# Layer 0's gate folded beside the projection's last queries, and all additions to the expert weights issued beside the attention

## The chip, the cores and the metric

The kernel runs on one core of a Trainium2 chip. Its metric is the device time of one execution in microseconds (us). Three runs of the kernel before took 980.25, 982.1 and 984.28 us; the median is 982.1. The engines are named as in the profile: PE is TensorE (PEld its weight loads), DVE is VectorE, ACT is ScalarE, POOL is GpSimd and SP is SyncE. A q behind a name (SPq, ACTq) is an engine's instruction queue, from which DMAs are issued.

## What is computed

Two transformer-like layers run over 8 batches of 256 tokens with 512 features, all in float32. This change lies in layer 0:

```python
# layer 0, attention: 8 heads of 64, 4 key/value groups, window of 256 keys, paged cache
q, k, v = x @ Wq.T, x @ Wk.T, x @ Wv.T          # RMS norm and rotation on q and k
k_blocks, v_blocks = cache with the 256 new rows of each batch written in
o = softmax(q k^T / 16, masked to the window) v
a = o @ Wo.T
# layer 0, feed-forward: top 2 of 8 experts
logits = clip(a @ gate_w.T, -50, 50)
rw = softmax(top 2 of logits)
weighted = (softmax(expert_atom_weights) @ atoms) * sigmoid(importance)   # 8 x 4096
out = a @ W.T + for each of 4096 places (row, col): out[row] += a[col] * sum_k rw_k * weighted[expert_k, place]
x = x + out
# layer 1: low-rank adapters on a linear layer, then a mixture of 8 GELU experts, added to x
```

Two rearrangements matter here. The logits are `o @ (Wo.T @ gate_w.T)`, so the kernel folds the gate through the output weights once (into `gwo`, 512 x 8) and multiplies attention outputs by that. And each expert's sparse update is added into a dense matrix of its own: `delta_d` in DRAM first receives W for all 8 experts, then the 4096 weighted values are added to it at their places, 128 places by one indirect DMA, 32 DMAs in all.

## The kernel before

**Order.** The program is written as Python loops; a list scheduler orders the instructions of each engine, by program order as their priority and by what is ready in its own model, so instructions of neighbouring steps interleave. Each engine then runs its list strictly in order, and waits at semaphores. A tile pool that is opened in memory of a closed one waits for the readers and writers of what lay there.

**Projection (L1147 to L1350).** PSUM is split into `psq` (3 banks) and `psd` (3 banks with tag psd, and one each for `pw0` and `pw1`). For 16 tiles of 128 tokens, `keys_values` multiplies (L1158), normalises and rotates keys and stores keys and values to `kv_new` (L1175). Beside it, `sum_same` (L1276) makes the values that are to be added to the weights (`sums`), and `find_places` their rows (`put_i`). From tile 8 on, six of the 32 additions are issued there, one to a tile (L1337, `add_delta` at L1127, on POOL). Loads of `wq`, `woT` and `gw` go through `later` (L1307), which writes one element of the tile from a late result, so that the load on SP can't run ahead. Then `gather_new(0)` fetches the new rows of batch 0, and the queries of batches 0 and 1 are made: `query_rows` (L1092, products at L1096) and `queries_turned` (L1114, transposes at L1121).

**Fold (L1490).** After the projection's pools are closed, each of four 128-column blocks of `woT` is transposed (L1497) and copied by ACT (L1499), and four products with 8 moving columns (`gw`) are accumulated (L1501). Four copies write `gwo` (L1509). It uses banks of the attention's pools.

**Attention (L1526 to L1568).** For batch b: the cache rows of batch b + 2 are gathered by POOL (4 DMAs from the old cache, 4 from `kv_new`, L1058), its queries are made (L1366, L1096, with a power on POOL at L1109 for `roots`), the sums in DRAM are started (L1520, L1523), and 128 queries attend (L1408 scores, L1423 mask and maximum, L1439 exponent, L1453 and L1457 transposes, L1462 values). Then `prepared` turns the keys of batch b + 1 (L1378, L1381) and builds its masks, five additions to `delta_d` are issued on POOL from `entries` (L1551 to L1561; one is left for batch 5), and the other 128 queries attend. `gate_rows` (L1479) and `output_rows` (L634) follow. In the last two batches the finished weights are read back (`raw`, L615) and laid out (L622).

**Layer 1** folds its gate with the helper `seen_through` (L114), which this change will use for layer 0 too. Its product is written as

```python
nc.tensor.matmul(
    acc[o * BW : (o + 1) * BW, :], gate[:, o, :], wn, start=True, stop=True
)
```

that is, 32 stationary columns (8 gates and zeros) and 512 moving ones; the four partial sums land in four groups of 32 partitions of one bank, which is copied, transposed and reduced by DVE (L134).

Of the kernel before, what the change touches and what calls it, by code (L numbers as in the profile page):

```python
# [11 lines left out]
F32 = mybir.dt.float32  # L12
# [7 lines left out]
P = 128  # L20
B, T, D = 8, 256, 512
# [3 lines left out]
KC = D // P  # L25
# [6 lines left out]
E = 8  # L32
# [3 lines left out]
NSC = NS // P  # L36
# [45 lines left out]
def two_layer_kernel(ctx: ExitStack, tc: tile.TileContext, io: dict, out: bass.AP):  # L82
    nc = tc.nc
# [14 lines left out]
    ident = const.tile([P, P], F32, name="ident")  # L98
# [4 lines left out]
    RK, BW = 16, 32  # L103
# [496 lines left out]
    woT = op.tile([P, KC, D], F32, name="woT")  # L600
    gwo = op.tile([P, KC, E], F32, name="gwo")
# [44 lines left out]
    with ExitStack() as att:  # L646
        ap = att.enter_context(tc.tile_pool(name="ap", bufs=1))
# [7 lines left out]
        sums = place_ap.tile([P, NSC, E], F32, name="sums")  # L655
# [9 lines left out]
        minus_half = ap.tile([P, 1], F32, name="minus_half")  # L665
        nc.gpsimd.memset(minus_half, -0.5)

        gw = ap.tile([P, KC, E], F32, name="gw")
        epss = ap.tile([P, 2], F32, name="epss")
        nc.gpsimd.memset(epss[:, 0:1], EPS)  # L670
        nc.gpsimd.memset(epss[:, 1:2], EPS / (SCALE * SCALE))
# [455 lines left out]
        def add_delta(k, values):  # L1127

            nc.gpsimd.indirect_dma_start(
                out=delta_d,  # L1130
                out_offset=bass.IndirectOffsetOnAxis(ap=put_i[:, k : k + 1], axis=0),
                in_=values,
                in_offset=None,
                bounds_check=D * D + P - 1,
                oob_is_err=True,
                compute_op=ALU.add,
            )
# [2 lines left out]

        roots = ap.tile([P, NT, H], F32, name="roots")

        BESIDE = 6
        LATER = 5


        with proj:  # L1147
# [3 lines left out]
            psd = proj.enter_context(tc.tile_pool(name="psd", bufs=3, space=PSUM))  # L1151
# [68 lines left out]
            for j in range(2):  # L1220
                for k in range(NSQ):
                    for h in range(2):
# [5 lines left out]
                            start=True,  # L1228
# [78 lines left out]
            def later(tile, src, rs):  # L1307

                nc.scalar.copy(tile[:, 0, :1], rs[:, :1])
                nc.sync.dma_start(tile, src)  # L1310

            FIRST = 8
            summed = placed = 0
            for i in range(LEAD, NT):
                rs = keys_values(i)
                if i == LEAD:
                    with_gains(qcos, qsin, "q_scale")
                    rot.close()
                base_weights(i)
                if i == 3:  # L1320
                    later(wq, wsrc[:, :, :512], rs)
                if i == 8:
                    later(woT, io["woT"].rearrange("(c p) o -> p c o", p=P), rs)
                    later(gw, io["gate0T"].rearrange("(c p) e -> p c e", p=P), rs)
                if i == 4:
                    find_blocks(psd, rs)
                if i in (6, 8, 10):
                    find_rows(i // 2 - 3)
                if i in (9, 11):
                    gather_old(i // 2 - 4)  # L1330
                for k in range(summed, min(summed + 3, NSC)):
                    sum_same(k)
                    summed = k + 1
                if summed - placed >= 8 or i == NT - 1:
                    find_places(range(placed, summed))
                    placed = summed
                if i >= FIRST and i - FIRST < BESIDE:  # L1337
                    add_delta(i - FIRST, sums[:, i - FIRST, :])
            gather_new(0)

            qq = proj.enter_context(tc.tile_pool(name="qq", bufs=2, side="right"))
            QTs = {}
            for b in range(2):
                rows = [
                    query_rows(
                        i, blocks[NTB][:, :, i * P : (i + 1) * P], psq, "pkv", qq, early=True
                    )
                    for i in range(2 * b, 2 * b + 2)
                ]
                QTs[b] = queries_turned(rows, psd, "psd")  # L1350


        otp = ost.enter_context(tc.tile_pool(name="otp", bufs=1, side="right"))
# [132 lines left out]
            nc.vector.tensor_scalar(lg0[:, i, :], pg, 50.0, -50.0, ALU.min, ALU.max)  # L1486

        AHEAD = 2

        with ExitStack() as fold:  # L1490
            fo = fold.enter_context(tc.tile_pool(name="fo", bufs=1))
            pgos = [ps_s.tile([P, 2, 512], F32, name="pgo", tag="ps") for j in range(KC // 2)]
            pgo = [pgos[k // 2][:, k % 2, :E] for k in range(KC)]
            for d in range(KC):
                pw = ps_o.tile([P, KC, P], F32, name="pw", tag="misc")
                for k in range(KC):
                    nc.tensor.transpose(pw[:, k, :], woT[:, k, d * P : (d + 1) * P], ident)  # L1497
                won = fo.tile([P, D], F32, name="won")
                nc.scalar.copy(won, pw.rearrange("p c r -> p (c r)"))  # L1499
                for k in range(KC):  # L1500
                    nc.tensor.matmul(  # L1501
                        pgo[k],
                        won[:, k * P : (k + 1) * P],
                        gw[:, d, :],
                        start=(d == 0),
                        stop=(d == KC - 1),
                    )
            for k in range(KC):
                nc.scalar.copy(gwo[:, k, :], pgo[k])  # L1509

        gather_new(1)
        ready = prepared(0, kv_rows[0])
        zero = wop.tile([P, D], F32, name="zero")
# [12 lines left out]
        for b in range(B):  # L1526
# [21 lines left out]
            now = ready  # L1548
            if b + 1 < B:
                ready = prepared(b + 1, kv_rows[b + 1])  # L1550
            ks = range(BESIDE + LATER * b, min(BESIDE + LATER * (b + 1), NSC))  # L1551
            if ks:

                held = bp.tile([P, 1], F32, name="held")
# [567 lines left out]
```

## Time and profile before

| | |
|---|---|
| median of three runs | 982.1 us (980.25 to 984.28) |
| profiled execution | 983.58 us, of which its span is 981.7 |
| mean granted TensorE clock | 0.967 |
| projection's last query product ends | 108.31 us |
| first scores of the attention | 133.42 us |
| last addition to `delta_d` issued | 313.0 us |
| additions issued by POOL | 6 from `sums` (94.2 to 116.1), 26 from `entries` (135.3 to 313.0) |

Times are microseconds from the start of the span of one profiled execution. "Busy" is what an engine worked; the bracket behind an instruction says how long its engine idled before it and which result ended the wait. The granted clock is TensorE's speed as a share of full speed. One float32 product shows as two records, a transpose as one. Instructions on PE are pipelined, so the distance between the starts of neighbours tells more than the length of one.

### The profile page before, as it was taken

The numbers are of one execution on the slowest core, as the hardware profiler recorded it, in microseconds if no ns is written. First come the engines' busy times: TensorE is split into PE (matmuls) and PEld (weight loads), VectorE is DVE, ScalarE is ACT, GpSimd is POOL, SyncE is SP. The second block draws the span as 40 slices with busy tenths as digits, with TensorE's granted clock in tenths as the row PEclk, the third lists the DMA queues.
The fourth block names the chain that finished last, engine by engine and source line by source line (L and its number), as shares of the span: only waits on it lengthen the run. The fifth ranks groups of instructions, "written<-read, shape, count | busy, mean of one in ns | idle before, by whom it ended". The sixth has DMA issues, their size and how long they took to land. (4 is left out here: it accounts for less than half of the span.)

```text
span 981.7 us, 14436 instructions
## 1 busy us (share of the span) xinstructions
PE 914.2 (93%) x4897; PEld 511.9 (52%) x4897; DVE 455.7 (46%) x1477; ACT 372.5 (38%) x958; POOL 357.2 (36%) x333
## 2 busy tenths in 40 slices
PE   6998889999999998897999997999599999999995
PEld 3554646556556565545433333545277777753332
DVE  5786789758548576583211111471012222323332
ACT  3675447547557489651111112410111111112321
POOL 2631655654554300123666652000223333333211
PEclk9898789999999999997999999999799999999998
DMA  6696494423441202256997766981433444343322
GB/s 192 216 320 236 123 306 143 115 59 82 118 126 28 93 19 70 84 195 226 344 308 139 126 111 144 357 315 43 171 74 67 70 73 73 65 75 62 49 28 37
DMA packets 74238, 134.63 MB, mean 137 GB/s; under 512 B 17309, under 2 KB 22941, under 8 KB 74032
## 3 DMA queue, kind: packets, MB, share of 16 engines
q0 software_dynamic: 25088, 43.68, 23.5%
q1 hardware_dynamic: 38496, 74.57, 21.9%
q10 hardware_dynamic: 10576, 15.39, 4.3%
q8 instruction: 42, 0.69, 0.3%
q14 instruction: 36, 0.29, 0.1%
HBM read 89.95 MB, written 52.56 MB: 145 GB/s over the span
## 5 line engine op out<-in xcount | busy, mean ns | idle before, releaser
L575 DVE COPY xsT<-pa 128x512 f32<-128x512 f32 x68 | 46.8, 688 | 155.6 <-PE pa L569 148.5
L533 POOL DMA_INDIRECT xs<-g_d,token_i_l x34 | 35.3, 1037 | 229.4 <-PE pa L569 129.4
L2014 DVE TENSOR_TENSOR y<-py,b 64x512 f32<-64x512 f32 (+1 forms) x46 | 31.7, 690 | 185.8 <-PE py L547 122.2
L1998 ACT ACTIVATE hs<-pu,b 128x64 f32<-128x64 f32 (+1 forms) x184 | 46.2, 348 | 185.8 <-PE pu L1972 144.4
L556 PE MATMUL py<-delta,xsT 128*64 128x512 f32 (+1 forms) x416 | 94.8, 598 | 0.0
L1439 ACT ACTIVATE s<-s,mx,roots 128x384 f32<-128x384 f32 x128 | 89.7, 705 | 12.2 <-DVE mx L1435 11.3
L1972 PE MATMUL pu<-xsT,w 128*128 128x128 f32 x704 | 82.9, 276 | 0.0
L1972 PEld LDWEIGHTS pu<-xsT,w 128*128 128x128 f32 x704 | 80.9, 193 | 0.4 <-issue 0.4
L547 PE MATMUL py<-w,hs 128*128 128x512 f32 x176 | 79.3, 593 | 0.0
L1158 PE MATMUL pkv<-wkv,xb 128*128 128x512 f32 x128 | 66.9, 648 | 8.5 <-DMA wkv<-wqkvT 8.5
L580 POOL DMA_INDIRECT out<-y,token_i_l x34 | 54.0, 1587 | 55.6 <-DVE y L2015 51.2
L1462 PE MATMUL po<-pT,kv 128*64 128x128 f32 x768 | 66.0, 283 | 7.1 <-ACT pT L1457 7.1
L1423 DVE CUSTOM_DVE_ANT_0 s<-ps,mask 128x384 f32<-128x384 f32 x128 | 67.1, 551 | 11.8 <-PE ps L1408 10.0
L1788 ACT ACTIVATE y<-py,weight_l 128x512 f32<-128x512 f32 x34 | 23.4, 688 | 126.1 <-PE py L556 86.9
L1462 PEld LDWEIGHTS po<-pT,kv 128*64 128x64 f32 x768 | 46.0, 136 | 43.1 <-ACT pT L1457 35.8
L580 POOL DMA_INDIRECT sums_d<-y,token_i_l x34 | 53.9, 1586 | 31.4 <-ACT y L1788 13.8
L1408 PE MATMUL ps<-KT,QT 64*128 64x384 f32 x256 | 59.1, 541 | 4.2 <-DVE mx L1423 4.0
L1457 ACT COPY pT<-pp 128x384 f32<-128x384 f32 x128 | 55.9, 478 | 16.7 <-PE pp L1453 15.8
L1453 PE MATMUL pp<-ident,s 128*128 128x128 f32 x384 | 59.9, 283 | 2.5 <-DVE s L1450 2.4
L569 PEld LDWEIGHTS pa<-ident,xs 128*128 128x128 f32 x272 | 32.7, 145 | 53.8 <-issue 48.4
L569 PE MATMUL pa<-ident,xs 128*128 128x128 f32 x272 | 43.6, 286 | 18.1 <-DMA xs<-g_d,token_i_l 11.4
L1096 PE MATMUL pq<-wq,xb 128*128 128x512 f32 x128 | 59.7, 614 | 0.0
(385 smaller groups left out, 1546.4 us busy)
## 6 DMA issues: line engine op xcount, KB each, us to landing
delta_d<-spread SPq DMA_DIRECT2D x16, 512.0 KB, 4.8
raw<-delta_d SPq DMA_DIRECT2D x16, 512.0 KB, 4.6
w<-fc_w SPq DMA_DIRECT2D x8, 1024.0 KB, 19.4
w<-fc_w SPq DMA_DIRECT2D x16, 512.0 KB, 17.3
part<-sums_d SPq DMA_DIRECT2D x32, 256.0 KB, 4.8
xb<-xT SPq DMA_DIRECT2D x5, 1024.0 KB, 6.4
sums_d<-zero SPq DMA_DIRECT2D x18, 256.0 KB, 5.4
kv_new<-kvt ACTq DMA_DIRECT2D x16, 256.0 KB, 2.7
```

The source lines that it names most:

```text
L547: nc.tensor.matmul(py, xT[:, k, :], of_expert(experts[0])(weights(k)), start=(k == 0), stop=(k == KC - 1),)
L556: lambda k=k, h=h: nc.tensor.matmul(py[h * HR : (h + 1) * HR, :], xT[:, k, h * HR : (h + 1) * HR], of_expert(experts[h])(weights(k)), star ...
L569: nc.tensor.transpose(dst[:, k, :], src[:, k * P : (k + 1) * P], ident)
L580: nc.gpsimd.indirect_dma_start(out=sum_d, out_offset=bass.IndirectOffsetOnAxis(ap=token_i[:, s : s + 1], axis=0), in_=y, in_offset=None, b ...
L1096: nc.tensor.matmul(pq, xcols[:, k, :], wq[:, k, :], start=(k == 0), stop=(k == KC - 1))
L1158: nc.tensor.matmul(pkv, xb[:, k, cols], wkv[:, k, :], start=(k == 0), stop=(k == KC - 1),)
L1408: lambda r=r: nc.tensor.matmul(pss[r], QT[r * HD : (r + 1) * HD, m, t * P : (t + 1) * P], KT[r * HD : (r + 1) * HD, u, t * P : t * P + WU] ...
L1423: nc.vector.tensor_tensor_reduce(out=s, in0=pss[r], in1=mask[:, t, :], scale=1.0, scalar=NEG, op0=ALU.add, op1=ALU.max, accum_out=mx[:, r ...
L1439: nc.scalar.activation(ss[r], ss[r], AF.Exp, bias=mx[:, r : r + 1], scale=root[:, r : r + 1], accum_out=sm[:, r : r + 1],)
L1453: nc.tensor.transpose(pp[:, c * P : (c + 1) * P], s[:, c * P : (c + 1) * P], ident)
L1462: lambda c=c, r=r: nc.tensor.matmul(po[r * HD : (r + 1) * HD, :], kvs[t + c][:, v0 + r * HD : v0 + (r + 1) * HD], pTs[r][:, c * P : (c + 1 ...
L1972: nc.tensor.matmul(pu[:, c, :], w1[:, k, plan.full[s], c * P : (c + 1) * P], xsT[:, k, :], start=(k == 0), stop=(k == KC - 1),)
```

## The change

`gw` is made 32 columns wide with zeros behind the 8 gates, and the load writes only the 8. The fold of L1490 is removed; `seen_through` is called in the projection's scope instead, after all query products of batches 0 and 1 and ahead of the turning of batch 1's queries. It uses the bank tagged `pw0` for its sums, the three `psd` banks for transposes, ACT for its copies and the pool `qq` for its SBUF tiles. The six additions of the projection loop are dropped there, and the attention's loop issues six to a batch from batch 0 on, so batches 0 to 4 take 30 and batch 5 the last two.

```diff
-        gw = ap.tile([P, KC, E], F32, name="gw")
+        gw = ap.tile([P, KC, BW], F32, name="gw")
+        nc.gpsimd.memset(gw, 0.0)
...
-        BESIDE = 6
-        LATER = 5
+        LATER = 6
...
-                nc.sync.dma_start(tile, src)
-
-            FIRST = 8
+                nc.sync.dma_start(tile[:, :, : src.shape[-1]], src)
+
...
-                if i >= FIRST and i - FIRST < BESIDE:
-                    add_delta(i - FIRST, sums[:, i - FIRST, :])
             gather_new(0)
 
             qq = proj.enter_context(tc.tile_pool(name="qq", bufs=2, side="right"))
-            QTs = {}
+            QTs, rows = {}, {}
             for b in range(2):
-                rows = [
+                rows[b] = [
...
-                QTs[b] = queries_turned(rows, psd, "psd")
+                if b == 0:
+                    QTs[b] = queries_turned(rows[b], psd, "psd")
+
+            seen_through(
+                gwo,
+                lambda o: [woT[:, k, o * P : (o + 1) * P] for k in range(KC)],
+                gw,
+                qq,
+                lambda name, shape: psd.tile(
+                    shape, F32, name=name, tag="pw0" if name == "acc" else "psd",
+                    bufs=1 if name == "acc" else 3,
+                ),
+                nc.scalar.copy,
+            )
+            QTs[1] = queries_turned(rows[1], psd, "psd")
...
-        with ExitStack() as fold:
-            fo = fold.enter_context(tc.tile_pool(name="fo", bufs=1))
-            pgos = [ps_s.tile([P, 2, 512], F32, name="pgo", tag="ps") for j in range(KC // 2)]
-            pgo = [pgos[k // 2][:, k % 2, :E] for k in range(KC)]
-            for d in range(KC):
-                pw = ps_o.tile([P, KC, P], F32, name="pw", tag="misc")
-                for k in range(KC):
-                    nc.tensor.transpose(pw[:, k, :], woT[:, k, d * P : (d + 1) * P], ident)
-                won = fo.tile([P, D], F32, name="won")
-                nc.scalar.copy(won, pw.rearrange("p c r -> p (c r)"))
-                for k in range(KC):
-                    nc.tensor.matmul(
-                        pgo[k],
-                        won[:, k * P : (k + 1) * P],
-                        gw[:, d, :],
-                        start=(d == 0),
-                        stop=(d == KC - 1),
-                    )
-            for k in range(KC):
-                nc.scalar.copy(gwo[:, k, :], pgo[k])
...
-            ks = range(BESIDE + LATER * b, min(BESIDE + LATER * (b + 1), NSC))
+            ks = range(min(LATER * b, NSC), min(LATER * (b + 1), NSC))
```

The helper that both folds now call:

```python
def seen_through(dst, blocks, gate, pool, banks, copy, **tags):
    acc = banks("acc", [P, D])
    for o in range(KC):
        pw = banks("pw", [P, KC, P])
        for k, src in enumerate(blocks(o)):
            nc.tensor.transpose(pw[:, k, :], src, ident)
        wn = pool.tile([P, D], F32, name="wn", **tags)
        copy(wn, pw.rearrange("p c r -> p (c r)"))
        nc.tensor.matmul(
            acc[o * BW : (o + 1) * BW, :], gate[:, o, :], wn, start=True, stop=True
        )
    parts = pool.tile([P, D], F32, name="parts", **tags)
    nc.scalar.copy(parts, acc)
    pt = banks("pt", [P, KC, P])
    for d in range(KC):
        nc.tensor.transpose(pt[:, d, :], parts[:, d * P : (d + 1) * P], ident)
    nc.vector.tensor_reduce(
        dst,
        pt.rearrange("p d (o c) -> p d c o", o=KC)[:, :, :E, :],
        AX.X,
        ALU.add,
    )
```

## The prediction, as it was made before the change was run

> **What bounds the kernel now.** I read first the table of busy time and the 40 slices, then windows over the stages, then the waits and the order of time around the one place the change moves.
>
> ```profile
> PE 914.2 (93%) x4897; PEld 511.9 (52%) x4897; DVE 455.7 (46%) x1477; ACT 372.5 (38%) x958; POOL 357.2 (36%) x333
> ...
> PEclk9898789999999999997999999999799999999998
> ```
>
> TensorE is busy 93% of the span, so time is won where TensorE idles or runs at a lowered clock. The clock row dips at the fifth slice (98 to 123 us). That is where the projection ends, the gate is folded (L1490 to L1509) and the attention has not begun. Windows of TensorE alone there (busy us, then granted clock, DMA share, GB/s):
>
> ```profile
> 108.00:110.00 2.00, 0.75 (x5) 1.00 0.35 42
> 110.00:112.00 2.00, 0.63 (x4) 0.86 1.07 358
> 112.00:114.00 2.00, 1.85 (x9) 0.50 0.98 331
> 122.00:124.00 2.00, 2.00 (x11) 0.50 0.58 152
> 126.00:128.00 2.00, 2.00 (x4) 0.50 0.98 280
> 128.00:130.00 2.00, 2.00 (x6) 0.88 1.02 343
> ```
>
> See two losses: from 108 to 112 TensorE does 1.4 us of work in 4, and from 111.5 to 128.3 it runs at clock 0.50. In order of time on TensorE:
>
> ```profile
> 104.71 3.60 PE L1096 MATMUL pq<-wq,xb 128*128 128x512 f32 x8
> 108.15 0.60 PE L1121 MATMUL pt<-ident,qr 128*128 128x128 f32 x4
> 110.84 0.63 PE L1121 MATMUL pt<-ident,qr 128*128 128x128 f32 x4 [2.10 <-DVE qr L1090]
> 112.15 1.97 PE L1497 MATMUL pw<-ident,woT 128*128 128x128 f32 x8 [0.68 <-ACT QT L1124]
> ...
> 124.43 9.05 PE L1096 MATMUL pq<-wq,xb 128*128 128x512 f32 x16
> 133.42 1.56 PE L1408 MATMUL ps<-KT,QT 64*128 64x384 f32 x8
> ```
>
> The last query product of the projection ends at 108.31 and the first scores start at 133.42: 25.1 us. Three parts: 3.8 us to the first transpose of the fold (mostly waits: batch 1's turned queries wait 2.10 for VectorE, the fold 0.68 for the copy that frees the projection's PSUM), 12.3 us of fold with 8 transposes of the keys (pk) among it, all at clock 0.50, and 9.0 us of batch 2's queries, the first 3.9 at 0.50. From 163 to 313 TensorE is busy 35.0 to 38.4 of 36 to 39 us a stage, so what the front gains is carried on.
>
> **The fold's work.** Removed: 16 transposes and 32 records of an 8-column product (16 matmuls, two passes each), four copies L1499, four L1509. At clock 0.50 a round (4 transposes, 8 records) takes 2.61 us (115.72 to 118.33), four 10.4. At full clock it would be 5.2, half of that. Added: the same transposes, four products of 512 columns on 32 stationary ones, one copy of the sum, four transposes, one reduction. The same helper already runs for layer 1, at clock 1.00:
>
> ```profile
> 606.58 1.05 PE L126 MATMUL acc<-wn,gw 128*32 128x512 f32 x4 [2.11 <-ACT wn L125]
> ...
> 609.76 1.05 PE L126 MATMUL acc<-wn,gw 128*32 128x512 f32 x2
> ...
> 611.11 1.05 PE L126 MATMUL acc<-wn,gw 128*32 128x512 f32 x2
> 612.89 0.66 PE L133 MATMUL pt<-ident,parts 128*128 128x128 f32 x4 [0.73 <-ACT parts L130]
> 613.93 1.09 PE L1839 MATMUL pt<-ident,part 128*128 128x128 f32 x8 [0.38 <-DVE gwc L134]
> ```
>
> One product alone holds TensorE 0.98 us (609.76 to 610.74); two side by side also 0.98 (606.58 to 607.57). So four cost 2.0 to 3.9, with 20 transposes at 0.116 (8 in 0.93, 151.92 to 152.85) 4.3 to 6.2 us: as much TensorE work as the old fold at full clock. Nothing is gained by the arithmetic; the gain must come from the place.
>
> The page "TensorE: Matmul & The Clock Gate" of the Trainium skill (section "Back-to-back issue gap") speaks against the new form: it gives 1 to 64 moving columns about 60 cycles and 512 about 518. By it four wide products (2072 cycles a pass) cost twice the sixteen narrow ones (960), about 0.9 us more over two passes at full clock (an estimate); the rows above give -1.4 to +0.5 us (2.0 to 3.9 against the 3.4 of half the 8-record stretch, 1.72, four times). I stay with the rows.
>
> **The new front, step by step, at full clock.** The transposes of woT need only woT (landed at 85) and a bank, so they fit the waits before 108.3 or follow it.
> - First round if nothing is hoisted: 0.46 transposes, about 0.2 wait, copy 0.59 (the L1499 row), 0.2 wait: first product at 109.7; if hoisted, 108.3.
> - Three rounds of 0.98 + 0.46 between first and last product: last one starts at 112.6 to 114.0. Batch 1's second query tile (ready at 110.7) is turned inside this, its waits covered.
> - Tail from the last product's start to the next user of TensorE: 2.82 us (611.11 to 613.93: copy, 4 transposes, reduction). The closing projection pool holds pk until then: 115.4 to 116.9.
> - pk 0.93: 116.4 to 117.8.
> - Batch 2's queries: their input is issued by SP at 108.46, just after the last read of the projection's block, and lands within 5.8 us (longest of that row): 114.3, so it does not hold them. 16 records take 7.13 us at full clock (row of 173.93). First scores at 123.5 to 124.9 against 133.42: **8.5 to 9.9 us earlier**.
>
> The keys of batch 0 must be there by 115.4. Now POOL interleaves their gathers with the six additions (107.83 to 115.63, pk at 120.94). Without these the four issues can follow the last kv_new write (issued 101.74, landing in 2.7): 4 x 1.36 from 104.5 ends at 110, plus 3.6 to land, 113.6. That is the place where taking the six additions away helps.
>
> Does the clock hold? The stretch from 108.3 to 111.7 holds 1.07 us of TensorE work and was followed by 0.50; 604.2 to 607.6 holds 1.29 of 3.4 and kept 1.00; the stretch from 134.8 to 138.2 holds 1.09 and lost it. The new front holds at least 4.7 us of work (4.3 and 0.46 for batch 1) in the 7.1 to 8.6 from 108.3: I take full clock. The same page (section "What's actually happening") says that the clock halves after at least one idle window of about 3.4 us and that the windows run free: the trace's 3.4 us agrees, and the page would let the new front hold as well.
> If it falls all the same, the second half of the fold (+2.0), pk (+0.9) and 3.9 us of queries at half rate (+1.9) give 4.8 back.
>
> VectorE caps the gain: from 133.4 to 163 it is the fullest engine.
>
> ```profile
> 108.00:133.40 25.40, 22.63 (x81) 15.82 (x79) 15.38 (x42) 5.38 (x13) 18.86 (x18) 0.66 0.73 210
> 133.40:163.00 29.60, 26.84 (x201) 16.13 (x200) 28.75 (x115) 23.15 (x61) 14.43 (x10) 0.94 0.82 260
> ```
>
> (columns: PE, PEld, DVE, ACT, POOL.) It idles 10.0 us in the first and 0.9 in the second, minus 0.29 for the new reduction: no more than 10.6 can be won. I keep 9.0.
>
> **The additions beside the attention.** Six go from L1338 to the loop at L1551, so batches 0 to 4 issue six instead of five and batch 5 two instead of one. On POOL each is 1.63 us and waits for the one before it to land: spacing 1.94 when a gather lies between, 3.4 alone, 6.65 at worst (135.25 to 141.90, DMA full). Behind them on POOL stand the gathers for two batches on and the powers for `roots`.
>
> ```profile
> POOL delta_d L1129 <- DMA delta_d<-entries,put_i: 25.0, 11, 4.0
> POOL kv L1058 <- PE po L1462: 13.1, 4, 3.8
> POOL roots L1109 <- DVE rs L1108: 15.4, 6, 6.2
> POOL delta_d L1129 <- DVE entries L1557: 10.9, 4, 3.7
> ```
>
> (us in all, times, longest, 133 to 350.) POOL arrives early by 3 to 4 us twice a batch from batch 2 on, so one addition more fits. In batches 0 and 1 POOL has no such slack (135 to 191 without a wait for another engine after 141.9), but it starts some 8 us earlier and what it makes is wanted late: batch 3's last gather is issued at 179.2 and first turned by TensorE at about 228.8, batch 4's 217.1 and 267.7: 49 us of cover. The first read of the finished weights goes from 316.2 to about 320, and its copy is at 363.2: covered. Cost 0; without cover 3.4 us a batch, six times, 20 us. Six fewer in the projection: TensorE never waited for them, 0. The wider gw costs one POOL fill near the start, like the 0.21 us of layer 1's at 406.8, beside other work; its load keeps its size. `find_places` and `entries` keep their place (48 columns for 40: under 0.1 us).
>
> **Sum.** The profiled execution took 983.58 (span 981.7, 1.9 around it). 983.6 - 9.0 = 974.6. It lay 1.5 above the median 982.1, so the median goes to 973.1; some of the fold's rounds may wait longer than I have it, so I say 974.
>
> **Rivals.**
> 1. The fold goes ahead of the last query products, so the block is read to its end 4.3 to 6.2 us later, batch 2's input with it (landing at 118.6 to 120.5), or the clock falls anyway. For: woT is ready at 85, and SP's load waits for the last reader. Against: the fold stands behind the queries in the program. 7.13 to 9.0 from there: 125.7 to 129.5, gain 4 to 7.7; with the fall of the clock 4.2. About 978. Chance 0.18.
> 2. Batch 0 is VectorE's (28.75 of 29.6), and an earlier TensorE waits there for its masks and maxima; or the fold is pushed to its old place by a bank it waits for. Gain 0 to 2: 981. Against: 10 us of VectorE idle just before. Chance 0.11.
> 3. **Slower.** POOL's queue, full in batches 0 and 1, takes the additions in a row at up to 6.65 us while DMA is full (0.82 of the stage), and never catches up, so the gathers hold the keys of each batch. It decides once POOL is over 45 us late; price 20 us less the 9 won: about 993. For: the 25.0 us it already waits for additions to land. Against: the idle it has from batch 2 on. Chance 0.13.
>
> **The numbers.** Forecast 0.58, rivals 0.18, 0.11, 0.13. A measurement here can tell 0.5% (4.9 us) from no change. Faster: 0.58 and nearly half of the first rival, 0.66; same 0.21; slower 0.13. Range: 12.6 us of gain (10.9 if the front has no gap: 13.8 us of work from 108.3 gives 122.5; and 1.7 if the second fall at 138 to 142 goes too) to the second rival's end with the spread of the runs shown: 969 to 985; only the slower case is left out.
>
> **What would show it.** Right: no 2 us window below 1.5 us busy between 108 and 116, clock 1.00 from 108 to 126, first scores near 124, stages from there to 313 as long as now, gathers still early. Wrong: 0.50 after 111, an SP load later than 109, or TensorE waiting for kv at L1378.

## The result, and the profile after it

The changed kernel takes 981.49 us (median of 20 runs, 974.46 to 987.96) where the kernel before takes 982.02 (20 runs, 979.08 to 989.39): ratio 0.998, 95% interval 0.9965 to 1.0001. That is no change; 974 was forecast. The experiments show where the gain went: the same kernel gains 0.6% on one chip (0.994, interval 0.991 to 0.997) and nothing on four other occasions, and the profiles differ in one place, by 5 us. Why that place differs stays open.

In the changed file lines move: products of the queries L1097, transposes of the queries L1122 and their copy L1125, keys L1389 (copy L1392), scores L1419, gathers L1059, additions L1130, load of xb L1377, xin L1509; the fold is the helper's L123 to L134. The profiled execution took 987.96 us, the slowest of the 20 (span 985.9); the front is read from it, not the total. TensorE's windows there (length, busy, granted clock, DMA share, GB/s):

```profile
110.00:112.00 2.00, 1.98 (x10) 1.00 0.63 180
112.00:114.00 2.00, 1.71 (x10) 1.00 1.05 369
114.00:116.00 2.00, 0.81 (x4) 1.00 1.00 326
116.00:118.00 2.00, 1.41 (x12) 1.00 0.80 244
118.00:120.00 2.00, 0.00 (x0) 1.00 0.65 215
120.00:122.00 2.00, 1.07 (x5) 0.61 0.95 346
122.00:124.00 2.00, 2.00 (x7) 0.50 0.92 261
```

The hole of before (108 to 112) is filled and the fold runs at clock 1.00. But a new hole stands behind the fold, and the clock falls after it. TensorE in order of time:

```profile
109.25 1.25 PE L123 MATMUL pw<-ident,woT 128*128 128x128 f32 x10
...
113.16 1.53 PE L126 MATMUL acc<-wn,gw 128*32 128x512 f32 x4 [0.29 <-issue]
115.88 0.66 PE L133 MATMUL pt<-ident,parts 128*128 128x128 f32 x4 [1.19 <-issue]
116.38 1.04 PE L1122 MATMUL pt<-ident,qr 128*128 128x128 f32 x8
120.93 1.97 PE L1389 MATMUL pk<-ident,kv 128*128 128x128 f32 x8 [3.52 <-ACT QT L1125]
122.89 9.29 PE L1097 MATMUL pq<-wq,xb 128*128 128x512 f32 x16
132.12 1.24 PE L1419 MATMUL ps<-KT,QT 64*128 64x384 f32 x6
```

I call **front** the time from the end of the first queries' products (here 109.25, where the fold starts) to the first scores: 22.9 us, against 25.1 before and 16.1 forecast. Of TensorE's 3.52 us of waiting, ScalarE's copies are named, and these waited as well:

```profile
119.51 0.59 ACT L1125 COPY QT<-pt 128x512 f32<-128x512 f32 x1 [3.68 <-remote]
120.29 0.59 ACT L1125 COPY QT<-pt 128x512 f32<-128x512 f32 x1 [0.19 <-remote]
```

TensorE began the eight transposes at 116.38; the first copy of their result began 3.1 us later. In the projection of the same run it begins 0.64 us later (106.24 to 106.88). VectorE's reduction of the fold's sums, whose transposes TensorE began at 115.88, waited as well:

```profile
118.06 0.29 DVE L134 TENSOR_REDUCE gwo<-pt 128x32 f32<-128x128 f32 x1 [3.14 <-PE pt L1122]
```

So it is not ScalarE that is slow. The trace also holds the times of TensorE's signals: 118.03, 119.49 and 120.26. Each of the three receivers starts 0.02 to 0.03 us after its signal. Either TensorE finished late or its signal came late; the trace can't tell these apart, since the ends of TensorE's records are modelled.

One more thing waits here, batch 0's keys. GpSimd's first gather

```profile
107.98 0.99 POOL L1059 DMA_INDIRECT kv<-kv_new,idx_new  x1 [31.35 <-DMA kv_new<-kvt]
```

waits for the last write of `kv_new` and the fourth is issued at 111.89. SyncE puts three loads of 0.5 MB beside them (xb 109.57, xin 110.01, xb 110.55), and the last packet recorded of the fourth gather lands at 118.2, not at 113.6.

So there were two suspects for the hole, the keys (**A**) and the late copies (**D**), and three others: the additions eat the gain behind GpSimd (**B**), the profile is a chance one (**C**), VectorE swallows the gain (**E**).

### The profile page after: what moved, and what is told of

It is laid out like the page before. It is cut to its first block, busy times and chain, and to the rows that moved or that the text cites. A ratio compares the mean times of both kernels' runs of the same rounds, so it can differ in the third digit from the quotient of the medians.

```text
span 985.9 us, 14396 instructions
## 1 busy us (share of the span) xinstructions
PE 917.0 (93%) x4877; PEld 508.1 (52%) x4877; DVE 453.7 (46%) x1476; ACT 373.0 (38%) x957; POOL 360.6 (37%) x334
## 3 DMA queue, kind: packets, MB, share of 16 engines
q0 software_dynamic: 25088, 43.68, 23.5%
## 5 line engine op out<-in xcount | busy, mean ns | idle before, releaser
L1158 PE MATMUL pkv<-wkv,xb 128*128 128x512 f32 x128 | 68.9, 665 | 8.5 <-DMA wkv<-wqkvT 8.5
L1130 POOL DMA_INDIRECT delta_d<-entries,put_i x32 | 52.8, 1651 | 50.9 <-DMA delta_d<-entries,put_i 41.8
L1419 PE MATMUL ps<-KT,QT 64*128 64x384 f32 x256 | 59.4, 544 | 3.3 <-DVE mx L1434 3.2
L1097 PE MATMUL pq<-wq,xb 128*128 128x512 f32 x128 | 60.1, 616 | 0.0
```

What stands on the lines that cost most here:

```text
L1097: nc.tensor.matmul(pq, xcols[:, k, :], wq[:, k, :], start=(k == 0), stop=(k == KC - 1))
L1158: nc.tensor.matmul(pkv, xb[:, k, cols], wkv[:, k, :], start=(k == 0), stop=(k == KC - 1),)
L1419: lambda r=r: nc.tensor.matmul(pss[r], QT[r * HD : (r + 1) * HD, m, t * P : (t + 1) * P], KT[r * HD : (r + 1) * HD, u, t * P : t * P + WU] ...
```

## The experiments

Times are medians; ratios are against the kernel before, run on the same chip, with 95% intervals. "Front" is read from the profile of each.

### The two halves of the change alone, and the change again

`adds_only` keeps the old fold and issues all 32 additions beside the attention; `fold_only` is the changed kernel with the additions as before:

```diff
-        LATER = 6
+        BESIDE = 6
+        LATER = 5
...
+                if i >= FIRST and i - FIRST < BESIDE:
+                    add_delta(i - FIRST, sums[:, i - FIRST, :])
...
-            ks = range(min(LATER * b, NSC), min(LATER * (b + 1), NSC))
+            ks = range(BESIDE + LATER * b, min(BESIDE + LATER * (b + 1), NSC))
```

`after_again` is the changed kernel.

> The changed kernel once more, for a second profile of it. Theory A (front): the fold runs at full clock from 109 to 116, but the turning of batch 0's keys cannot start before about 121, TensorE idles some 3.5 us ahead of it, its clock falls to 0.50 for about 6.8 us, and the first scores come 1 to 2 us earlier than the kernel before. Ratio 0.998 to 1.000. Rival B (additions): the front is won by 5 us or more in most runs and lost again in batches 0 to 5 behind POOL; then this trace shows the lead of the first scores over 4 us and a smaller one at the rows of batch 5. Rival C (chance): the profile of the result was an unlucky one; then the wait ahead of the keys is under 1 us here.

> The early fold with the additions left as before (six in the projection, five to a batch). Theory A: the keys of batch 0 are gathered between additions as before, so they are turned at about 121 again; ratio 0.997 to 1.001, first scores within 1.5 us of the changed kernel. Rival B: free of the sixth addition it is faster than the changed kernel by 2 to 5 us (ratio 0.993 to 0.996).

> The late fold as before, with all 32 additions beside the attention. Theory A: POOL has room, so within 1 us of the kernel before (ratio 0.999 to 1.001), and the rows of batch 5 at the same time. Rival B: slower by 2 to 5 us (1.002 to 1.005), with TensorE waiting for keys or roots in batches 1 to 4.

Measured: the change again 980.8 us, 0.999 (0.997 to 1.002), front 25.5; the additions alone 983.8, 1.000 (0.997 to 1.003), front 25.3; the fold alone 984.4, 1.002 (0.9995 to 1.005), front 26.3. So the moved additions cost nothing that an interval of 0.3% shows, and B falls. C falls too: in the second profile of the changed kernel TensorE waits 4.27 us ahead of pk. On GpSimd of the changed kernel, from 133 to 350 us (what waited, total, times, longest):

```profile
POOL delta_d L1130 <- DMA delta_d<-entries,put_i: 41.8, 17, 5.6
...
POOL roots L1110 <- DVE rs L1109: 8.1, 2, 6.2
...
POOL kv L1059 <- PE po L1473: 6.0, 3, 3.3
POOL delta_d L1130 <- DVE entries L1546: 5.1, 3, 2.5
```

It waits 17 us more for additions than before (41.8 against 25.0), and 20 us less for the other engines, whom it had been ahead of; no TensorE wait for keys or `roots` follows. The fold alone is another matter. There the additions still stand between the gathers (103.7 is the start of the fold):

```profile
112.05 0.33 PE L1393 MATMUL pk<-ident,kv 128*128 128x128 f32 x1 [0.73 <-DVE posb L1400]
116.60 0.48 PE L1393 MATMUL pk<-ident,kv 128*128 128x128 f32 x1 [4.21 <-DMA kv<-kv_new,idx_new]
118.53 0.48 PE L1393 MATMUL pk<-ident,kv 128*128 128x128 f32 x1 [1.45 <-DMA kv<-kv_new,idx_new]
119.97 1.33 PE L1393 MATMUL pk<-ident,kv 128*128 128x128 f32 x5 [0.96 <-DMA kv<-kv_new,idx_new]
```

TensorE waits 6.6 us for keys. The early fold can pay only if the additions leave the gathers' way; the two halves belong together, as forecast (`fold_late_sums` below shows it where the early fold does pay).

### Holding the clock by filler

Four unread products in the kernel before, ahead of the turning of batch 1's queries:

```diff
+                if b == 1:
+                    for j in range(4):
+                        idle = psq.tile([P, D], F32, name="idle", tag="pkv")
+                        nc.tensor.matmul(
+                            idle, woT[:, j, :P], woT[:, j, :], start=True, stop=True
+                        )
```

> The kernel before with four products of 128x512 whose results nothing reads, in the wait between the last query product and the turned queries of batch 1. They cost at most 0.8 us on TensorE. Theory A (the clock is the price of the old place): the clock stays at 1.00 through the fold, which takes 5 to 6 us instead of 10.4, the keys are turned between 117 and 121 and the first scores come 3 to 6 us earlier; ratio 0.994 to 0.997. If the clock falls anyway, or the keys of batch 0 hold the queries, ratio 0.999 to 1.001.

Measured: 989.2 us, 1.008 (1.005 to 1.010), slower, though the front fell to 23.5 us and the clock held to 118.8. The four products took TensorE 3.4 us (106.64 to 110.08), not the 0.8 expected; most of that is time in which it waits in the kernel before. The gain was lost behind it: from the pk of batch 1 to that of batch 5 it takes 160.5 us (148.9 to 309.4), the kernel before 154.7 (151.9 to 306.6). The scheduler had put the attention's instructions in another order. An edit at the front must be judged with the order behind it.

### Keys, loads, order of the turning

`keys_free` takes batch 0's fresh rows from the cache; `late_sums` starts the first batch's sums one batch later; `turned_first` turns batch 1's queries ahead of the fold; `turned_late_sums` does both.

```diff
-            gather(b, kv_new, idx_new, N)
+            gather(b, kv_new if b else io["cache"], idx_new, N)      # keys_free
...
-            if b < B - 2:
+            if b == 1:
+                start_sums(0)                                        # late_sums
+            if 0 < b < B - 2:
                 start_sums(b)
...
-                if b == 0:                                           # turned_first
-                    QTs[b] = queries_turned(rows[b], psd, "psd")
+                QTs[b] = queries_turned(rows[b], psd, "psd")
```

> The changed kernel, with the fresh rows of batch 0's keys and values taken from the cache in place of kv_new: the transfers stay as large and as many, but batch 0 leaves out its new keys and waits for no write of kv_new. TensorE's, VectorE's and ScalarE's orders are those of the changed kernel. Theory A (the front is held by the arrival of batch 0's keys): the gathers are issued about 30 us earlier, pk at L1389 starts as soon as batch 1's queries are turned, at 116.5 to 117.5; no idle window opens, the granted clock stays 1.00 through the queries of batch 2 (from about 119) and the first scores start 15 to 17 us after the last product of the first queries, not 23 to 26; if nothing later gives it back the kernel takes 973 to 976 us. Theory D (the hold is ScalarE's late copies of batch 1's turned queries, whatever the keys do): pk still starts at 120 to 121 with a wait on ScalarE's copy at L1125, the clock still falls at 119 to 121, the time stays at 980 to 982. Theory E (the front shrinks, but batches 0 to 2 are held by VectorE and swallow it): first scores 6 to 9 us earlier, but the gates of token block 4 on start less than 2 us earlier than in the changed kernel and the time stays at 979 to 982.

> The changed kernel with the first batch's start of the sums (xin loaded, written, and two rows of zeros) issued one batch later, so that one load less of 0.5 MB lies between batch 2's input and batch 0's gathers. Theory A, by contention (the keys come late because the gathers share the transfers with three loads): the last gather of batch 0 lands by about 115 rather than 118, TensorE's wait ahead of pk shrinks from 3.5 to under 1 us, the clock stays 1.00, 974 to 977 us. Theory A, by the write of kv_new (the gathers are issued only at 108 and the loads matter little): the last gather lands at 116 to 118, pk at 118 to 120, 979 to 982 us. Theory D (ScalarE's late copies for another reason): gathers earlier, pk at 120 to 121 still, 980 to 982 us.

> The changed kernel with batch 1's queries turned before the fold, as in the kernel before; the fold stands between them and batch 0's keys. Theory D (the copies of the turned queries are what pk waits for): the copies are done by about 112 and pk waits for the gathers alone, starting at about 118 in place of 120.6; 979 to 981 us. Theory A (keys): pk starts when the last gather has landed, 117.5 to 118.5, so a wait of 1 to 2 us stays behind the fold with the gathers as its releaser, the clock falls in that window or not; first scores 21 to 25 us after the last product of the first queries; 978 to 982 us.

> Both edits of the two runs before it: batch 1's queries turned before the fold, and the first start of the sums one batch later. If keys and late copies are both needed for the wait, and contention is what makes the keys late, pk starts right behind the fold at 115 to 116.5, the clock stays 1.00, the first scores start 15 to 17 us after the last product of the first queries, 973 to 976 us. If the write of kv_new alone sets the keys, pk starts at 116.5 to 118 and the time is 978 to 982 us. If the rest of the order pays for the shift of the sums, the front shrinks and the time does not: 979 to 983 us, and the loss is in the batches behind the first.

Measured: `keys_free` front 17.0 us, the clock at 1.00 from 33 to 402 us, the first gate 9.8 us earlier than in the result's profile (152.2 against 162.0) and the first of the last batch 10.5 (398.5 against 409.0), which is the shorter front and a projection that ended 3.8 us earlier, so E falls: nothing swallows the front. Its total, 1042 us, says nothing: from 592 us on it is 62 us longer than the changed kernel from 601 on (446 us against 384), presumably since other keys send later tokens to other experts. `late_sums` 974.4 us, 0.992 (0.989 to 0.996), front 17.1: the forecast time. `turned_first` 980.7, 0.999 (0.996 to 1.002), front 19.0; `turned_late_sums` 983.0, 1.000 (0.997 to 1.003), front 19.0; both lose behind it, from the pk of batch 1 to that of batch 5, 158.8 and 159.2 us where the changed kernel takes 155.8, since the order is altered there.

It looked as if `late_sums` had removed the cause, but it still puts three loads into the front (xb, xb, xin at 104.1 to 105.1), and no copy was late in any of the four profiles. They were taken on another chip than the four before. So two new theories: SyncE's order decides (**F**), or the chip does (**G**).

### The changed kernel and the moved start side by side

`before_late_sums` and `fold_late_sums` put the same edit into the kernel before and into `fold_only`.

> The changed kernel once more, on the same chip as the moved start of the sums. Theory F (SyncE's order ahead of the first batch decides: the load of xin between the two inputs makes TensorE run slowly from about 112 us and its hand-overs late): 979 to 983 us, the first scores 23 to 26 us after the last product of the first queries, batch 1's turned queries copied at 118 to 120.5, 2 us or more after TensorE issued them. Theory G (the state of the chip in a run decides and the moved sums were lucky, since the runs with late copies were all on another chip): as fast as with the moved sums, 973 to 976 us, the first scores 17 us after.

> The changed kernel with the first start of the sums one batch later, once more. TensorE's and VectorE's instructions are in the order of the changed kernel. Theory F: 973 to 976 us again, first scores 17 to 18 us after the last product of the first queries, clock at 1.00 through batch 2's queries. Theory G: in half of the runs as slow as the changed kernel; median 977 to 981 us.

> The kernel before with the first start of the sums one batch later and nothing else. Theory F: the front of the kernel before is held by the late fold and TensorE's wait ahead of it, so the moved sums alone are worth little: 979 to 983 us, first scores 24 to 26 us after the last product of the first queries. If the moved sums alone bring the 7 us (a rival, H: the gain has nothing to do with the fold): 973 to 976 us.

> The early fold with the additions to the weights left as in the kernel before (six beside the projections), and the first start of the sums one batch later. POOL's gathers of batch 0 stand between the additions there, the last issued at 116.5. Theory: the additions must go from in front of the gathers for the fold to pay; 981 to 985 us, TensorE waits for the gathers ahead of pk (1 us or more), first scores 22 us or more after the last product of the first queries. Rival: SyncE's order was all, and this is as fast as the moved sums with all 32 additions beside the attention, 973 to 976 us.

Measured on this third chip: **the changed kernel 974.4 us, 0.994 (0.991 to 0.997)**, front 17.3; `late_sums` again 973.9, 0.992 (0.989 to 0.996), front 17.0; the edit in the kernel before 983.2, 1.002 (0.999 to 1.005), front 25.3; with the fold alone 985.3, 1.003 (0.999 to 1.006), front 25.6, with TensorE's waits for keys as above. F falls, H (the moved sums alone) too: the unaltered change has its forecast time here. TensorE, ScalarE and VectorE in it:

```profile
105.33 1.25 PE L123 MATMUL pw<-ident,woT 128*128 128x128 f32 x10
...
109.24 1.53 PE L126 MATMUL acc<-wn,gw 128*32 128x512 f32 x4 [0.29 <-ACT wn L125]
111.45 0.66 PE L133 MATMUL pt<-ident,parts 128*128 128x128 f32 x4 [0.68 <-ACT parts L130]
111.94 1.04 PE L1122 MATMUL pt<-ident,qr 128*128 128x128 f32 x8
113.70 1.42 PE L1389 MATMUL pk<-ident,kv 128*128 128x128 f32 x8 [0.73 <-ACT QT L1125]
115.54 7.13 PE L1097 MATMUL pq<-wq,xb 128*128 128x512 f32 x16 [0.42 <-DVE KT L1392]
122.61 1.56 PE L1419 MATMUL ps<-KT,QT 64*128 64x384 f32 x8
```

```profile
112.58 1.07 ACT L1125 COPY QT<-pt 128x512 f32<-128x512 f32 x2 [1.18 <-PE pt L1122]
```

```profile
112.14 0.29 DVE L134 TENSOR_REDUCE gwo<-pt 128x32 f32<-128x128 f32 x1 [1.14 <-PE pt L133]
```

The first copy begins 0.64 us after the transposes, the reduction 0.69 us after its own (2.2 in the result's profile). Set beside the result's rows: from the fold's start to the queries' transposes 6.6 us here and 7.1 there; from there to pk 1.8 and 4.6; pk to pq 1.8 and 2.0; pq to the scores 7.1 and 9.2. The 5.6 us between the two fronts are thus 2.8 of late hand-over, 2.2 of half clock in pq and 0.6 of small change. The last packets of batch 0's fourth gather land at 114.3, 9.0 us after the fold's start; in the result's profile 8.9. The keys are equally late in both, so A is not what makes the difference. They cost 0.3 us here (pk takes 1.42, 1.09 where nothing holds it).

Part 6 of the pages shows which profile is of which kind. In the result's, landing times are missing:

```profile
kv_new<-kvt ACTq DMA_DIRECT2D x16, 256.0 KB
```

and in the one with the 17.3 us front they are there:

```profile
kv_new<-kvt ACTq DMA_DIRECT2D x16, 256.0 KB, 3.0
```

That row lacks its time in the result's profile, in those of the first four runs, and in none of the eight that followed; the profile of before, from which the forecast was made, has it. Signals are lost where it is missing: the result's trace holds 9,611 of them, that of the 974.4 us run 10,652. The changed kernel was slow where it is missing. I call chips whose profiles lack it chips of the first kind.

### On chips of the first kind

> The changed kernel, beside the moved start of the sums on the same chip. If SyncE's order decides (F): slow, 979 to 983 us, wherever hand-overs are late, with the moved sums at 973 to 976 us beside it. If the chip or the occasion decides (G): within 2 us of the moved sums, both at 973 to 977 us or both at 979 to 983 us.

> The changed kernel with the first start of the sums one batch later, beside the changed kernel. F: 973 to 976 us whatever the changed kernel does. G: within 2 us of the changed kernel.

Measured, with landing times missing in both: 980.3 us, 0.999 (0.996 to 1.002), front 23.6, first copy of the turned queries 2.8 us after TensorE began them; and 980.0, 0.997 (0.994 to 1.001), front 20.9, copy 1.8 us after. G holds, with the medians 0.3 us apart; G names the chip or the occasion, and the runs don't separate the two.

The next kernels hold transfers back: a load's tile first gets one element from the turned queries (`quiet_loads`: batch 2's and 3's inputs and the first xin; `hold_two`: without batch 2's input); `quiet_both` also makes the indices of batch 1's fresh gathers late.

```diff
             xb = xq.tile([P, KC, T], F32, name="xb", bufs=3)
+            if b < 4:                                   # hold_two: if b == 3
+                nc.scalar.copy(xb[:, 0, :1], QTs[1][:, 0, T - 1 :])
...
+            if b < 1:
+                nc.scalar.copy(xin[:, 0, :1], QTs[1][:, 0, T - 1 :])
...
+        nc.vector.tensor_scalar(after_qt, QTs[1][:, 0, T - 1 :], -1e30, None, ALU.is_lt)  # quiet_both
+        nc.vector.tensor_scalar(idx_new[:, 1, :], idx_new[:, 1, :], after_qt, None, ALU.add)
         gather_new(1)
```

> The changed kernel with the loads of batch 2's and batch 3's inputs and the first xin held until ScalarE has copied batch 1's turned queries (ScalarE writes one element of each tile first). The gathers stay. If the loads delay the hand-overs: the copies of the turned queries come 1.1 to 1.3 us after TensorE begins them (as in the profiles with no late hand-over), on a chip that loses signals as well; pk follows within 1 us of the copies or waits for the last gather. If they do not: copies 2.5 us or more late on such a chip. On a chip that loses none the copies are on time in any case and the run tells nothing of this. The total says little: batch 2's queries wait for an input that is issued 8 us later and then lands 3 to 4 us later, so TensorE waits ahead of pq and the clock falls there: 980 to 988 us.

> As the run before, with batch 1's fresh gathers held behind the turned queries as well (their indices have a zero added that is worked out from the turned queries). Beside the fold only batch 0's four gathers move. If transfers delay the hand-overs, on a chip that loses signals the copies are on time here even if they were late with the loads alone held; if it is the chip's TensorE itself, they are late by 1 to 3 us here too. Total 980 to 990 us.

> The changed kernel with the first xin and batch 3's input held until ScalarE has copied batch 1's turned queries; batch 2's input is loaded as in the changed kernel. If the loads beside the fold are what delays hand-overs and keys: batch 0's last gather lands 6 to 7 us after the fold begins (9 in the changed kernel), the copies of the turned queries are on time or under 1 us late, the first scores come 16 to 18 us after the last product of the first queries, and the time is 972 to 976 us on any chip. If one load is enough to delay them, or the clock falls anyway on such a chip: 978 to 982 us.

> The changed kernel beside it on the same chip. On a chip whose traces lose signals: 979 to 983 us with copies of the turned queries 2 to 4 us late; on one that loses none: 973 to 976 us with copies on time.

All four profiles lack landing times. `quiet_loads` and `quiet_both` ran on a chip where the changed kernel was not run; only `hold_two` has it beside it. The changed kernel, on the chip of `hold_two`: 980.4 us, 0.999 (0.997 to 1.002), front 23.2, transposes at 113.58 and

```profile
116.46 0.59 ACT L1125 COPY QT<-pt 128x512 f32<-128x512 f32 x1 [3.42 <-remote]
119.29 0.59 ACT L1125 COPY QT<-pt 128x512 f32<-128x512 f32 x1 [2.25 <-remote]
```

`hold_two` beside it, transposes at 112.61, with one wait of 1.42 inside the fold:

```profile
109.91 1.53 PE L126 MATMUL acc<-wn,gw 128*32 128x512 f32 x4 [1.42 <-issue]
...
116.70 7.13 PE L1097 MATMUL pq<-wq,xb 128*128 128x512 f32 x16 [0.59 <-DVE KT L1394]
```

```profile
113.25 0.59 ACT L1125 COPY QT<-pt 128x512 f32<-128x512 f32 x1 [1.18 <-PE pt L1122]
114.38 0.58 ACT L1125 COPY QT<-pt 128x512 f32<-128x512 f32 x1 [0.55 <-PE pt L1122]
```

The first copy follows after 0.64 us, the second 0.55 late. The wait inside the fold is a late hand-over too: ScalarE copied `wn` at 109.27, 1.65 us after TensorE began its transposes, where the result's profile has 0.53. The fourth gather, as far as its landings are recorded, is there at 110.1, 5.2 us after the fold's start; the clock stays 1.00 to 128; the front is 18.9 (16 to 18 was expected). With all three loads held (`quiet_loads`) the first copy follows after 0.64 us and the second is 0.44 late, with the gather 5.6 us after the fold's start. With batch 1's gathers held too (`quiet_both`) both copies are on time:

```profile
112.17 1.04 PE L1122 MATMUL pt<-ident,qr 128*128 128x128 f32 x8
113.94 1.09 PE L1391 MATMUL pk<-ident,kv 128*128 128x128 f32 x8 [0.73 <-issue]
```

On the one chip with a neighbour, then, fewer loads went with less delay. That transfers are the cause is not shown, and two rows speak against it. In `quiet_both` other transfers had moved up, four gathers of cache rows (issued from 109.78 to 113.72) and writes of zeros to the sums (from 109.64). Its copies are on time at a DMA share of 0.92; the result's profile has them late at 0.80 (116 to 118):

```profile
111.00:113.00 2.00, 1.32 (x13) 1.00 0.92 235
```

The next hand-over there, of pk to VectorE, was late: 2.4 us after TensorE began pk (113.94 to 116.37), against 0.8 in `late_sums` again. And `adds_only`, on a chip of the first kind, has the three loads (108.40 to 109.38) and the eight gathers (104.44 to 114.53) beside its old fold, and its copies are on time at a share of 1.01 (113 to 122), with the clock at 0.50.

The totals do not pay: `quiet_loads` 986.5 (1.006, 1.002 to 1.010) and `quiet_both` 985.7 (1.005, 1.001 to 1.008), where pq waits for its late input as expected; `hold_two` 980.9 us, 0.998 (0.995 to 1.001), not its expected 972 to 976. Its first gate is 7.4 us earlier than its neighbour's (153.5 and 160.9) and the first of the last batch 3.5 (403.6 and 407.1). The rest is lost from the pk of batch 1 to that of batch 5, 159.4 us against 154.9. Here TensorE and VectorE keep their neighbour's order, so the order is not the reason. Most of the loss is one more late hand-over:

```profile
181.60 1.25 PE L1475 MATMUL po<-pT,kv 128*64 128x128 f32 x12 [1.99 <-ACT pT L1470]
```

ScalarE began that copy at 181.07, 2.6 us after the last of the transposes it waited for (178.49), and the clock was 0.50 from 183.2 to 186.6.

## Why the prediction was wrong

**Right where no hand-over was late.** Its terms against the changed kernel's 974.4 us run: front 16.1 forecast, 17.3 measured, a gain of 7.8 where 9.0 was taken; fold's start to pk 7.1 to 8.6 forecast, 8.4 measured; pq 7.13, measured 7.07; gain carried on: that profile's span is 10.8 us under that of before, as are its first scores, 7.8 from the front and 3.0 from a projection that ran ahead because the clock didn't fall at 81 us as it does in the profile of before. By the ratio the gain there is 0.6%, some 6 us. Of this chip there is one run of the changed kernel.

**The step that failed** in the result is "The closing projection pool holds pk until then: 115.4 to 116.9". pk came at 120.9, 11.7 us after the fold's start, where the forecast has 7.1 to 8.6. The term is the tail, from the last product of the fold to pk: 2.82 us forecast, 7.3 measured (113.65 to 120.93). Two things were wrong in it. The forecast had batch 1's second query tile turned inside the fold with its waits covered; the transposes of both tiles, eight in all, stand behind it, and pk waits for their copies. That alone makes the tail 4.0 us in the 974.4 us run (109.73 to 113.70), where the time from the fold's start to pk still stays inside its bounds (8.4). And the 2.82 had been read off layer 1's fold at 611 us, which took for granted that TensorE's results reach the next engine as fast in the new place. In the result's profile they came 2.8 us late. A full DMA is not enough for that: layer 1's fold runs at DMA share 1.02 in the same profile (the last but one figure of the first line) and waits 0.73, as before.

```profile
612.00:614.00 2.00, 2.00 (x6) 0.34 (x4) 0.69 (x1) 0.00 (x0) 0.00 (x0) 1.00 1.02 345
```

```profile
614.75 0.66 PE L133 MATMUL pt<-ident,parts 128*128 128x128 f32 x4 [0.73 <-ACT parts L130]
```

**The second step, "I take full clock"**, fell with the first: TensorE idles from 117.41 to 120.93, and the clock is 0.50 from 120.4 to 127.3. The page "TensorE: Matmul & The Clock Gate" of the Trainium skill (section "What's actually happening") has the clock halved after at least one idle window of about 3.4 us. The trace comes close but is milder: the clock fell 3.0 us into the idle time, and the 3.4 us before the fall still held 0.4 us of TensorE's work. The forecast's own stretches give no bound: they reach past the falls, and the 3.4 us right before the falls of the kernel before at 111.43 and 138.73 hold 1.31 and 1.39 us, no less than the 1.29 that kept 1.00. Hand-over and clock together took 5.0 of the 7.8 us. The forecast had priced the fall alone (4.8 us back, rival 1), but tied it to a thin front, not to a late signal behind a full one.

**The keys "there by 113.6"** was wrong in both profiles of the changed kernel set side by side above, by about 4 us from the fold's start: the last write of `kv_new` took 4.2 us to land (103.03 to 107.2), not 2.7, and three loads were in flight beside the gathers, which the sum had left out. It cost 0.3 us in the 974.4 us run, because the fold's tail covered it; a shorter fold would have waited for the keys.

**Confirmed:** the additions cost nothing measurable (1.000) and had to leave the gathers' way; the fold's TensorE work is about unchanged and the place is what counts; batch 2's input (113.0) holds nothing; the load of 109.57 us, called a sign of failure if later than 109, is no sign of it: it comes 0.3 us after the fold's start, as in the 974.4 us run (105.65 and 105.33). **Rivals:** 1 came closest, by its "or the clock falls anyway"; 2 falls (`keys_free` carried its whole front on); 3 falls (`adds_only`).

**Open:** why TensorE's results come late, why on some chips or occasions and not on others, and whether the recording, whose losses go with it, has a part in it. The unedited kernel before takes 980.2 to 982.3 us on both kinds, and the old fold's copies are on time on a chip of the first kind (`adds_only`, 113.29 to 121.11). Why the clock falls at 81 us in some profiles was not tried. The best version found is `late_sums`, which leaves TensorE's order alone (974.4, 973.9 and 980.0 us on three chips, the changed kernel 974.4 and 980.3 beside the last two); that it beats the changed kernel is not shown.

## What to carry to other kernels

A front that is filled to the last microsecond depends on every hand-over in it; list what else moves at that moment, and price a late signal with the clock that falls behind it. Before explaining a missing gain by the code, run the unaltered change again on several chips: here the chip or the occasion decided between 0.999 and 0.994, and the edit that first seemed to cure it had only been run elsewhere. A move at the front also lets the scheduler reorder everything behind it, so compare the pace of later batches before judging an edit.

## What the hardware showed that was not expected

Between chips that run the kernel before equally fast, the time from TensorE's transposes to the copy of their result differed by more than a factor of four in the same program (0.64 us against 2.8 to 3.2). The receivers were not slow: ScalarE and VectorE started 0.02 to 0.03 us after TensorE's recorded signal. It is not bound to the front either, as the copy at 181.07 in `hold_two` shows. The traces that show it are those that lack landing times. And the granted clock stood at 1.00 while TensorE's results came late (116 to 120 in the result's profile): the lost time shows in the waits of the engines alone.
